# Attention projections: values of two pairs of heads by seven half-depth products, and a pair's last block closed inside the next projection

## The chip, the cores and the metric

The kernel runs on one core of one Trainium2 chip. The metric is the device time of one execution in microseconds (us): before the change the median of three runs is 3855.34 (3853.4 to 3857.73). All arithmetic is f32. The core's engines work side by side, each through its own instructions in order, and wait for each other through semaphores: TensorE (PE in the profile, its weight loads PEld), VectorE (DVE), ScalarE (ACT), GpSimd (POOL) and SyncE (SP, which issues most DMAs).

## The reference, cut to what matters

Four layers of the form x = x + layer(groupnorm(x)) on a 512 x 64 x 64 image: one attention layer, two gated convolution layers, one linear attention. Only the first is touched:

```python
x = x + _L0_conv_ref(_gn(x), wq, wk, wv, wo)

q = to_tokens(_conv1x1(fmap, wq, gain_in))   # 8 heads x 4096 tokens x 64
k = to_tokens(_conv1x1(fmap, wk, gain_in))
v = to_tokens(_conv1x1(fmap, wv, gain_in))
AA = jnp.sum(q * q, axis=-1)
qk = jnp.einsum('bid,bjd->bij', q, k)
sim = -(AA[:, :, None] + AA[:, None, :] - 2.0 * qk) * scale
attn = jax.nn.softmax(sim, axis=-1)
out = jnp.einsum('bij,bjd->bid', attn, v)
return _conv1x1(out.reshape(...), wo, gain_out)
```

## The kernel before

X, the 512 channels x 4096 tokens, stays in SBUF as four chunks of 128 channels. `_attention_pairs` does the eight heads as four pairs; a pair's 2 x 64 channels fill the 128 partitions. Tokens come in NB = 8 blocks of BLK = 512. For each pair there is a projection, `project`, and then the attention proper, block by block.

**Projection.** Four repeats k, of two blocks each, make Q and K of the pair (128 channels x 512 tokens a block). Weights (Q matrix a, K matrix b) times two blocks of X would be eight products of half the depth (256 channels, so two matmuls of 128 x 128 on 512 columns each). `_Seven` does it with seven, in Strassen's manner (Winograd's form): `sums` makes four sums of the two weight matrices (s[0] to s[3]) once a pair, `differences` four differences of the X blocks (t[0] to t[3], eight instructions of VectorE, L450) in every repeat, and `steps` gives the seven products p1, p5, p2, p7, p6, p3, p4 with their evictions. p1 and p5 open PSUM banks 0 and 1 and are copied by ScalarE into "kept" tiles (L620); p2 and p3 go on adding in the same banks; p7 and p6 use banks 2 and 3, p4 adds to 2. VectorE makes five adds a repeat: kept[1] with p7 (L483), kept[0] with p6 (L487), and three that write Q and K (L647); ScalarE writes the fourth quarter (L645). Banks 0 and 1 lie in the pool `ps_av` and 2 and 3 in `ps_s` (three buffers, one of which is taken by `ps_a` during a projection). The "row" tiles (kept, and avs and rd of the attention) have three buffers, the "pt" tiles (differences, squares, the exponentials) five, the "acc" tiles (weight sums, the fourth difference, the running sums of exponentials) two.

The pair's values are made plainly, turned with tokens on the partitions: `value(b)` (L604) multiplies 128-token slices of X, as the loaded operand, by the pair's value weights (128 columns that stream), 4 slices x 4 chunks = 16 matmuls a block, and ScalarE copies the block to V (L611). `squares` (L627) sums Q squared for AA into `ps_a`; at the end of a projection VectorE transposes it (L674) into A, the bias of the exponentials.

**Attention.** For each block b, 32 key tiles t: `scores` (four 64 x 64 matmuls, L693, and two exponentials on ScalarE, L701), and two tiles later `values` (L713) while VectorE adds the tile into acc (L778). After the last tile avs is gathered from two PSUM tiles av0 and av1 (L783, L788). `close` sums acc over the keys by TensorE (ps_d, L722), takes the reciprocal (L726), writes the normalized output over Q (L727) and checks the sums (L728, L731). A block is closed early in the next block, but a pair's last one right after its loop, ahead of the next projection.

The order on each engine is made by the tile framework's scheduler, by its own estimates; a tile's buffer is handed on when its last reader is through. Weights of a pair (wqkv, L576, one DMA) are loaded when the pair before has finished its projection, and scaled by the normalization's gain (L395 on GpSimd; in pair 0 on VectorE and ScalarE).

Of the kernel before, what the change touches and what calls it, by code (L numbers as in the profile page):

```python
# [143 lines left out]
def _all(pieces):  # L144
    for _ in pieces:
        pass
# [269 lines left out]
class _Seven:  # L416
# [22 lines left out]
    def differences(self, eng, x, t):  # L439

        for j, (a, b) in enumerate(
# [7 lines left out]
            for c in range(2):  # L449
                yield eng.tensor_tensor(t[j][c], a(c), b(c), ALU.subtract)  # L450

    def steps(self, a, b, s, t, x, bank, keep, put):

# [5 lines left out]
        def add(j, w, hs, first):  # L459

            if first:
                ps[j] = bank(j)
            for c in range(2):
                self.matmul(
                    ps[j], w[:, c], hs[c], start=(first and c == 0), stop=(c == 1),
                    skip_group_check=not first,
                )

# [28 lines left out]

        return [p1, p5, p2, p7, p6, p3, p4]


# [7 lines left out]
def _attention_pairs(tc, a, X, QO, gmask, small, centered, stats, mv, okay):  # L508
# [19 lines left out]
    with tc.tile_pool(name="att1", bufs=1) as p1, tc.tile_pool(  # L528
# [34 lines left out]
        K = p1.tile([P, N], FP, tag="K", name="K")  # L563
        V = p1.tile([P, NT, P], FP, tag="V", name="V")
        A = p1.tile([P, NT, 2], FP, tag="A", name="A")
# [6 lines left out]

        def project(pair):

            w = p1.tile([P, 3, NC, P], FP, tag="wqkv", name=f"wqkv{pair}")
            nc.sync.dma_start(out=w, in_=a["L0_wqkv"][pair])  # L576
            for n in range(3):
                centered.scaled(
                    w[:, n], gains[:, min(n, 1)],
                    nc.gpsimd if pair else nc.scalar if n else nc.vector,  # L580
                )
            if pair == 0:
                centered.began()
            Q = QO[pair]
            psa = ps_s.tile([P, 2 * BLK], FP, tag="s", name="ps_a")
            wsum = p2.tile([P, 2 * BLK], FP, tag="acc", name="w_sum").rearrange(
                "p (n c m) -> p n c m", n=4, c=2
            )
            wsum = [wsum[:, n] for n in range(4)]
            sums = seven.sums(nc.vector, w[:, 0], w[:, 1], wsum)  # L590

            def differences(k):
                tiles = [ptp.tile([P, 2 * BLK], FP, tag="pt", name="diff") for _ in range(3)]
                tiles.append(p2.tile([P, 2 * BLK], FP, tag="acc", name="diff"))
                t = [[t[:, ts(c, BLK)] for c in range(2)] for t in tiles]
                return t, seven.differences(
                    nc.vector, lambda c, n: X[:, c, ts(2 * k + n, BLK)], t
                )

            def value(b):  # L600
                ps = ps_s.tile([P, 2 * BLK], FP, tag="s", name="ps_v")[:, 0:BLK]
                for i in range(QT):
                    for c in range(NC):
                        nc.tensor.matmul(  # L604
                            ps[:, ts(i, P)],
                            X[:, c, ts(b * QT + i, P)],
                            w[:, 2, c, :],
                            start=(c == 0),
                            stop=(c == NC - 1),
                        )  # L610
                nc.scalar.copy(V[:, ts(b, QT), :].rearrange("p t d -> p (t d)"), ps)  # L611

            def bank(j):
                if j < 2:
                    return ps_av.tile([P, BLK], FP, tag=f"av{j}", name="ps7")
                return ps_mm.tile([P, BLK], FP, tag="mm", name="ps7")

            def keep(j, ps):
                t = p3.tile([P, BLK], FP, tag="row", name="kept")
                nc.scalar.copy(t, ps)  # L620
                return t

            def squares(k, sq):

                sq = sq.rearrange("p (t j k) -> p j t k", j=4, k=32)
                for j in range(4):
                    nc.tensor.matmul(  # L627
                        psa[ts(j, 32), ts(k, 256)].rearrange("p (t k) -> p t k", k=32),
                        halves,
                        sq[:, j],  # L630
                        start=True,
                        stop=True,
                    )

            late = []
            for k in range(NB // 2):
                if pair == 0:
# [4 lines left out]
                def put(m, n, ps, more):  # L642
                    dst = (K if m else Q)[:, ts(2 * k + n, BLK)]
                    if more is None:
                        nc.scalar.copy(dst, ps)  # L645
                    else:
                        nc.vector.tensor_add(dst, ps, more)  # L647
# [24 lines left out]
            late.pop(0)()  # L672
            at = ptp.tile([P, 2 * BLK], FP, tag="pt", name="at")
            nc.vector.transpose(at, psa)  # L674
            nc.vector.tensor_copy(A, at.rearrange("p (t k) -> p t k", k=32)[:, :, 0:2])
# [31 lines left out]

        def values(av, t, pt):
            for half in range(2):
                keys = slice(half * D, (half + 1) * D)  # L710
                for h in range(2):
                    rows = slice(h * D, (h + 1) * D)
                    nc.tensor.matmul(  # L713
                        av[half][rows, :], V[keys, t, rows], pt[keys, ts(h, BLK)],
                        start=(t == 0), stop=(t == NT - 1),
# [34 lines left out]
        for pair in range(HEADS // 2):  # L750
            project(pair)
            if pair == HEADS // 2 - 1:
# [7 lines left out]
            for b in range(NB):  # L760
# [5 lines left out]
                for t in range(NT + AHEAD):  # L766
# [4 lines left out]
                    if t >= AHEAD:  # L771
                        u = t - AHEAD
                        pt = pts.pop(u)
                        values(av, u, pt)
                        if u == 0:
# [1153 lines left out]
```

## Time and profile before

| | |
|---|---|
| median of three runs | 3855.34 us |
| the profiled execution | 3857.97 us, span 3856.2 us |
| granted TensorE clock | 0.997 of full |
| TensorE busy in the span | 3774.7 us, 98% |
| projection of pair 0, of pairs 1 to 3 | about 34 to 116 us; 567.7 to 647.6, 1098.3 to 1178.2, 1629.0 to 1708.9 us |
| attention of pairs 0 to 3 | between these, about 450 us each, the last to about 2250 with the output projection |
| VectorE and ScalarE busy from 566 to 648 us | 37.0 and 16.8 us of 82 |
| the three later layers | about 2274 to 3856 us |

The page gives for each group of instructions its line, engine, output and inputs, count, busy time, mean duration, and the idle time of the engine just before them with what ended it. In a timeline a row is the start in us, the length in us, and the instructions run together. Each f32 matmul leaves two matmul records and two weight load records. Matmul lengths overlap, so the pace is read from the starts.

### The profile page before, as it was taken

What the parts mean: (1) busy time and instruction counts of PE and PEld (TensorE: products, weight loads), DVE (VectorE), ACT (ScalarE), POOL (GpSimd) and SP (SyncE); (2) the same over time, 40 slices, a digit from 0 to 9 for tenths busy, and PEclk for the clock granted to TensorE, in tenths of its full rate; (3) what the DMA queues carried; (4) which work ended last, traced back from release to release, by engine and by line L of the source; (5) the groups of instructions that cost most, each with busy time, mean ns of one, the idle gap of its engine ahead of it and who ended that gap; (6) DMA issues with size and microseconds to landing.
All of it is one profiled execution on the core that took longest, in us unless ns stands there. A gap on an engine that the chain in (4) does not pass through costs nothing. (4 is left out here: it accounts for less than half of the span.)

```text
span 3856.2 us, 81818 instructions
## 1 busy us (share of the span) xinstructions
PE 3774.7 (98%) x35446; PEld 1675.2 (43%) x35446; DVE 2645.7 (69%) x3214; ACT 2067.8 (54%) x2994; POOL 108.6 (3%) x92
## 2 busy tenths in 40 slices
PE   6999999999999999999999999999999999999999
PEld 4533335333354333353333334554444544455544
DVE  5677774777766787747776757767677677575535
ACT  3677763777736777636565655663246632354210
POOL 0000000000000000000000000000000000121100
PEclk9999999999999999999999999999999999999999
DMA  2000000000000000000000015763047730563334
GB/s 99 10 1 1 1 1 9 1 1 1 1 1 9 1 1 1 1 9 1 1 1 1 1 49 161 202 197 84 13 156 193 202 97 27 154 183 92 94 97 140
DMA packets 194012, 221.56 MB, mean 57 GB/s; under 512 B 13400, under 2 KB 138584, under 8 KB 193520
## 3 DMA queue, kind: packets, MB, share of 16 engines
q1 hardware_dynamic: 166832, 157.12, 15.0%
q10 hardware_dynamic: 26784, 59.11, 4.2%
q8 instruction: 280, 4.59, 0.5%
q14 instruction: 84, 0.69, 0.1%
q0 software_dynamic: 32, 0.06, 0.0%
HBM read 156.46 MB, written 59.77 MB: 56 GB/s over the span
## 5 line engine op out<-in xcount | busy, mean ns | idle before, releaser
L701 ACT ACTIVATE pt<-ps_s,A 128x512 f32<-128x512 f32 x2048 | 1286.3, 686 | 534.9 <-PE ps_s L693 527.3
L778 DVE TENSOR_TENSOR acc<-acc,pt 128x1024 f32<-128x1024 f32 x960 | 1178.2, 1227 | 323.5 <-ACT pt L701 296.0
L713 PE MATMUL av<-pt,V 64*64 64x512 f32 x8192 | 1112.6, 590 | 0.9 <-ACT pt L701 0.9
L693 PE MATMUL ps_s<-O,K 64*64 64x512 f32 x8192 | 1111.7, 589 | 0.0
L713 PEld LDWEIGHTS av<-pt,V 64*64 64x64 f32 x8192 | 339.8, 133 | 557.1 <-issue 525.3
L693 PEld LDWEIGHTS ps_s<-O,K 64*64 64x64 f32 x8192 | 334.2, 133 | 554.0 <-issue 307.0
L952 ACT COPY S<-S 32x1295 f32<-32x1295 f32 (+1 forms) x272 | 341.5, 1256 | 219.0 <-DMA S<-F 114.4
L879 PEld LDWEIGHTS ps_cv<-S,T 64*32 64x32 f32 x13824 | 194.0, 105 | 111.1 <-issue 78.7
L879 PE MATMUL ps_cv<-S,T 64*32 64x128 f32 x13824 | 232.6, 273 | 5.8 <-issue 2.1
L879 PE MATMUL ps<-diff,w_sum 128*128 128x512 f32 x492 | 231.7, 602 | 3.1 <-DVE w_sum L437 1.9
L879 PE MATMUL ps<-h,w_out_L 128*128 128x512 f32 x512 | 229.6, 599 | 1.5 <-DVE X L1233 1.4
L450 DVE TENSOR_TENSOR diff<-X 128x512 f32<-128x512 f32 x200 | 133.5, 684 | 73.6 <-PE ps L879 46.9
L879 PE MATMUL ps<-X,w_in_L 128*128 128x512 f32 x304 | 147.1, 615 | 13.3 <-ACT kept L1155 6.3
L383 ACT ACTIVATE X<-X,gn_less 128x512 f32<-128x512 f32 x122 | 77.1, 708 | 152.1 <-DVE gn_less L125 152.1
L879 PEld LDWEIGHTS ps<-h,w_out_L 128*128 128x128 f32 x512 | 94.0, 190 | 118.3 <-issue 96.5
L879 PE MATMUL ps<-h,pw_L 128*128 128x512 f32 x320 | 143.8, 599 | 1.4 <-DVE h L1221 1.1
L1006 DVE STREAM_TRANSPOSE h<-ps_cv 128x512 f32<-128x512 f32 x112 | 109.1, 1047 | 51.4 <-PE ps_cv L879 51.1
L450 DVE TENSOR_TENSOR diff<-X,diff 128x512 f32<-128x512 f32 x200 | 133.6, 683 | 11.6 <-PE ps L879 10.8
L879 PEld LDWEIGHTS ps<-diff,w_sum 128*128 128x128 f32 x492 | 90.3, 190 | 111.4 <-issue 101.5
L604 PEld LDWEIGHTS ps_v<-wqkv,X 128*128 128x128 f32 x1024 | 119.5, 193 | 18.0 <-issue 12.5
L604 PE MATMUL ps_v<-wqkv,X 128*128 128x128 f32 x1024 | 120.8, 276 | 0.0
L483 DVE TENSOR_TENSOR kept<-kept,ps 128x512 f32<-128x512 f32 x57 | 38.9, 682 | 115.8 <-ACT sq L668 77.6
(182 smaller groups left out, 3135.4 us busy)
## 6 DMA issues: line engine op xcount, KB each, us to landing
T<-in_L_T_dram SPq DMA_DIRECT2D x112, 384.0 KB, 4.3
F<-plane ACTq DMA_DIRECT2D x112, 324.0 KB, 3.6
S<-F SPq DMA_DIRECT2D x224, 162.0 KB, 4.5
row<-G SPq DMA_DIRECT2D x80, 272.0 KB, 3.6
S<-G SPq DMA_DIRECT2D x96, 153.0 KB, 4.2
G<-plane ACTq DMA_DIRECT2D x48, 289.0 KB, 2.3
T<-in_L_T_dram SPq DMA_DIRECT2D x48, 256.0 KB, 3.9
out_dram<-y SPq DMA_DIRECT2D x32, 256.0 KB, 2.0
```

The source lines that it names most:

```text
L383: self.nc.scalar.activation(xs, xs, AF.Identity, bias=less)
L450: yield eng.tensor_tensor(t[j][c], a(c), b(c), ALU.subtract)
L483: nc.vector.tensor_add(kept[1], kept[1], ps[2])
L604: nc.tensor.matmul(ps[:, ts(i, P)], X[:, c, ts(b * QT + i, P)], w[:, 2, c, :], start=(c == 0), stop=(c == NC - 1),)
L693: nc.tensor.matmul(ps[ts(half, D), ts(h, BLK)], K[rows, t * P + half * D : t * P + (half + 1) * D], QO[pair][rows, cols], start=True, stop ...
L701: exp = nc.scalar.activation(pt[:, ts(h, BLK)], ps[:, ts(h, BLK)], AF.Exp, bias=A[:, t, h : h + 1])
L713: nc.tensor.matmul(av[half][rows, :], V[keys, t, rows], pt[keys, ts(h, BLK)], start=(t == 0), stop=(t == NT - 1),)
L778: add = nc.vector.tensor_add(acc, acc if u > 1 else first, pt)
L879: self.tc.keep_in_program_order(self.nc.tensor.matmul(*args, **kw))
L952: nc.scalar.copy(second, first)
L1006: nc.vector.transpose(out, src)
```

## The change

- For an even pair the projection makes the values of this pair and the next at once. Two value weight matrices (2 x 128 output channels) on two blocks are again a two by two scheme, so a class `_SevenTurned` runs the same seven steps with the operands swapped: slices of X or of its differences are loaded, weights or their sums stream, 4 x 2 = 8 matmuls of 128 columns a product. Its weight sums lie in the last 1024 columns of the pair's own Q buffer until Q is written there. An odd pair makes no values.
- The values of even pairs lie in QO[3], which is free until pair 3's Q is written; those of odd pairs in V.
- The X differences have one set of tiles a projection, used by both groups of seven and made for repeat k + 1 during the last group of repeat k. Banks 0 and 1 lie in `ps_s` now and 2 and 3 in `ps_av`. `ps_a` is taken after the first repeat.
- Weights come in DMAs of one matrix each; the second value matrix lies in the buffer of the later `wo` tile.
- `close` of a pair's last block is called within the next `project`, after the second product of its first group (except for the last pair, where nothing changes).

The diff, cut to its core:

```diff
+    def multiply(self, ps, w, hs, first):
+        for c in range(2):
+            self.matmul(
+                ps, w[:, c], hs[c], start=(first and c == 0), stop=(c == 1),
+                skip_group_check=not first,
+            )
...
-            for c in range(2):
-                self.matmul(
-                    ps[j], w[:, c], hs[c], start=(first and c == 0), stop=(c == 1),
-                    skip_group_check=not first,
-                )
+            self.multiply(ps[j], w, hs, first)
...
+class _SevenTurned(_Seven):
+    def multiply(self, ps, w, hs, first):
+        for i in range(BLK // P):
+            for c in range(2):
+                self.matmul(
+                    ps[:, ts(i, P)], hs[c][:, ts(i, P)], w[:, c],
+                    start=(first and i == c == 0), stop=(c == 1), skip_group_check=True,
+                )
...
-        def project(pair):
...
+        def home(pair):
+            return V if pair % 2 else QO[NC - 1]
+        def project(pair, meanwhile=None):
             w = p1.tile([P, 3, NC, P], FP, tag="wqkv", name=f"wqkv{pair}")
-            nc.sync.dma_start(out=w, in_=a["L0_wqkv"][pair])
-            for n in range(3):
+            w = [w[:, n] for n in range(3)] + [p1.tile([P, NC, P], FP, tag="wo", name="wv")]
+            src = [(pair, 0), (pair, 1), (pair, 2), (pair + 1, 2)][: 2 if pair % 2 else 4]
+            for n, (p, m) in enumerate(src):
+                nc.sync.dma_start(out=w[n], in_=a["L0_wqkv"][p][:, m])
+            for n in range(len(src)):
                 centered.scaled(
-                    w[:, n], gains[:, min(n, 1)],
-                    nc.gpsimd if pair else nc.scalar if n else nc.vector,
+                    w[n], gains[:, n // 2 if n > 1 else n],
+                    nc.gpsimd if pair else nc.vector if n in (2, 0) else nc.scalar,
                 )
...
-            wsum = p2.tile([P, 2 * BLK], FP, tag="acc", name="w_sum").rearrange(
-                "p (n c m) -> p n c m", n=4, c=2
-            )
-            wsum = [wsum[:, n] for n in range(4)]
-            sums = seven.sums(nc.vector, w[:, 0], w[:, 1], wsum)
+            def matrices(t):
+                t = t.rearrange("p (n c m) -> p n c m", n=4, c=2)
+                return [t[:, n] for n in range(4)]
+            sums = matrices(p2.tile([P, 2 * BLK], FP, tag="acc", name="w_sum"))
+            made = [(w[0], w[1], sums, seven.sums(nc.vector, w[0], w[1], sums))]
+            if pair % 2 == 0:
+                sums = matrices(Q[:, N - 2 * BLK :])
+                made.insert(0, (w[2], w[3], sums, seven.sums(nc.vector, w[2], w[3], sums)))
+            tiles = [ptp.tile([P, 2 * BLK], FP, tag="pt", name="diff") for _ in range(3)]
+            tiles.append(p2.tile([P, 2 * BLK], FP, tag="acc", name="diff"))
+            diff = [[t[:, ts(c, BLK)] for c in range(2)] for t in tiles]
+            def view(k):
+                return lambda c, n: X[:, c, ts(2 * k + n, BLK)]
             def differences(k):
-                tiles = [ptp.tile([P, 2 * BLK], FP, tag="pt", name="diff") for _ in range(3)]
-                tiles.append(p2.tile([P, 2 * BLK], FP, tag="acc", name="diff"))
-                t = [[t[:, ts(c, BLK)] for c in range(2)] for t in tiles]
-                return t, seven.differences(
-                    nc.vector, lambda c, n: X[:, c, ts(2 * k + n, BLK)], t
-                )
-            def value(b):
-                ps = ps_s.tile([P, 2 * BLK], FP, tag="s", name="ps_v")[:, 0:BLK]
-                for i in range(QT):
-                    for c in range(NC):
-                        nc.tensor.matmul(
-                            ps[:, ts(i, P)],
-                            X[:, c, ts(b * QT + i, P)],
-                            w[:, 2, c, :],
-                            start=(c == 0),
-                            stop=(c == NC - 1),
-                        )
-                nc.scalar.copy(V[:, ts(b, QT), :].rearrange("p t d -> p (t d)"), ps)
+                if pair == 0:
+                    for b in (2 * k, 2 * k + 1):
+                        for c in range(NC if b else 0):
+                            centered.take(X[:, c, ts(b, BLK)], c)
+                return seven.differences(nc.vector, view(k), diff)
...
             def bank(j):
                 if j < 2:
-                    return ps_av.tile([P, BLK], FP, tag=f"av{j}", name="ps7")
-                return ps_mm.tile([P, BLK], FP, tag="mm", name="ps7")
+                    return ps_mm.tile([P, BLK], FP, tag="mm", name="ps7")
+                return ps_av.tile([P, BLK], FP, tag=f"av{j - 2}", name="ps7")
...
+            def put(dst, n, ps, more):
+                d = dst[:, ts(n, BLK)]
+                if more is None:
+                    nc.scalar.copy(d, ps)
+                else:
+                    nc.vector.tensor_add(d, ps, more)
+            late, psa = [], []
+            pieces = differences(0)
...
-                    for b in (2 * k, 2 * k + 1):
-                        for c in range(NC if b else 0):
-                            centered.take(X[:, c, ts(b, BLK)], c)
...
-                t, pieces = differences(k)
-                steps = seven.steps(
-                    w[:, 0], w[:, 1], wsum, t, lambda c, n: X[:, c, ts(2 * k + n, BLK)],
-                    bank, keep, put,
-                )
-                value(2 * k)
-                if k:
-                    late.pop(0)()
-                for _ in range(4):
-                    next(sums, None)
-                    next(pieces)
-                    next(pieces)
-                for step in steps[:5]:
-                    step()
-                value(2 * k + 1)
-                for step in steps[5:]:
-                    step()
+                after = iter(())
+                for g, (wa, wb, ws, sums) in enumerate(made):
+                    values = g + 1 < len(made)
+                    dst = [home(pair), home(pair + 1)] if values else [Q, K]
+                    steps = (turned if values else seven).steps(
+                        wa, wb, ws, diff, view(k), bank, keep,
+                        lambda m, n, ps, more: put(dst[m], 2 * k + n, ps, more),
+                    )
+                    for n, step in enumerate(steps):
+                        if n == 0:
+                            next(sums, None)
+                            next(pieces, None)
+                            next(pieces, None)
+                        if n == 1:
+                            _all(sums)
+                            _all(pieces)
+                        step()
+                        if n == 1 and meanwhile:
+                            meanwhile()
+                            meanwhile = None
+                        if n == 3 and late:
+                            late.pop()()
+                        if not values and n == 2 and k + 1 < NB // 2:
+                            pieces = differences(k + 1)
+                        for _ in range(0 if values else {2: 2, 5: 4}.get(n, 0)):
+                            next(pieces, None)
+                if not psa:
+                    psa.append(ps_s.tile([P, 2 * BLK], FP, tag="s", name="ps_a"))
...
-            project(pair)
+            project(pair, pair and (lambda: close(*done)))
...
             if pair == HEADS // 2 - 1:
                 output(NB - 2, range(2))
-            close(*done)
+                close(*done)
```

More of the change, by code (lines that the diff above doesn't have):

```diff
@@ L563, in _attention_pairs @@
         K = p1.tile([P, N], FP, tag="K", name="K")
-        V = p1.tile([P, NT, P], FP, tag="V", name="V")
+        V = p1.tile([P, N], FP, tag="V", name="V")
         A = p1.tile([P, NT, 2], FP, tag="A", name="A")
@@ L571, in _attention_pairs @@
         seven = _Seven(tc, nc.tensor.matmul)
-        def project(pair):
+        turned = _SevenTurned(tc, nc.tensor.matmul)
+        def home(pair):
+            return V if pair % 2 else QO[NC - 1]
+        def project(pair, meanwhile=None):
             w = p1.tile([P, 3, NC, P], FP, tag="wqkv", name=f"wqkv{pair}")
-            nc.sync.dma_start(out=w, in_=a["L0_wqkv"][pair])
-            for n in range(3):
+            w = [w[:, n] for n in range(3)] + [p1.tile([P, NC, P], FP, tag="wo", name="wv")]
[3 more added lines that the diff above has]
+            for n in range(len(src)):
                 centered.scaled(
-                    w[:, n], gains[:, min(n, 1)],
-                    nc.gpsimd if pair else nc.scalar if n else nc.vector,
+                    w[n], gains[:, n // 2 if n > 1 else n],
+                    nc.gpsimd if pair else nc.vector if n in (2, 0) else nc.scalar,
                 )
@@ L584, in project @@
             Q = QO[pair]
-            psa = ps_s.tile([P, 2 * BLK], FP, tag="s", name="ps_a")
-            wsum = p2.tile([P, 2 * BLK], FP, tag="acc", name="w_sum").rearrange(
-                "p (n c m) -> p n c m", n=4, c=2
-            )
-            wsum = [wsum[:, n] for n in range(4)]
-            sums = seven.sums(nc.vector, w[:, 0], w[:, 1], wsum)
-            def differences(k):
-                tiles = [ptp.tile([P, 2 * BLK], FP, tag="pt", name="diff") for _ in range(3)]
-                tiles.append(p2.tile([P, 2 * BLK], FP, tag="acc", name="diff"))
-                t = [[t[:, ts(c, BLK)] for c in range(2)] for t in tiles]
-                return t, seven.differences(
-                    nc.vector, lambda c, n: X[:, c, ts(2 * k + n, BLK)], t
-                )
@@ L627, in squares @@
                     nc.tensor.matmul(
-                        psa[ts(j, 32), ts(k, 256)].rearrange("p (t k) -> p t k", k=32),
+                        psa[0][ts(j, 32), ts(k, 256)].rearrange("p (t k) -> p t k", k=32),
                         halves,
@@ L633, in squares @@
                     )
-            late = []
-            for k in range(NB // 2):
-                if pair == 0:
-                    for b in (2 * k, 2 * k + 1):
-                        for c in range(NC if b else 0):
-                            centered.take(X[:, c, ts(b, BLK)], c)
[L642 to L647, printed above, removed]
-                t, pieces = differences(k)
-                steps = seven.steps(
-                    w[:, 0], w[:, 1], wsum, t, lambda c, n: X[:, c, ts(2 * k + n, BLK)],
-                    bank, keep, put,
-                )
-                value(2 * k)
-                if k:
-                    late.pop(0)()
-                for _ in range(4):
-                    next(sums, None)
-                    next(pieces)
-                    next(pieces)
-                for step in steps[:5]:
-                    step()
-                value(2 * k + 1)
-                for step in steps[5:]:
-                    step()
@@ L671, in project @@
                 late.append(lambda k=k, sq=sq: squares(k, sq))
-            late.pop(0)()
+            late.pop()()
             at = ptp.tile([P, 2 * BLK], FP, tag="pt", name="at")
-            nc.vector.transpose(at, psa)
+            nc.vector.transpose(at, psa[0])
             nc.vector.tensor_copy(A, at.rearrange("p (t k) -> p t k", k=32)[:, :, 0:2])
@@ L706, in scores, with values @@
             return pt
-        def values(av, t, pt):
+        def values(v, av, t, pt):
             for half in range(2):
@@ L713, in values @@
                     nc.tensor.matmul(
-                        av[half][rows, :], V[keys, t, rows], pt[keys, ts(h, BLK)],
+                        av[half][rows, :],
+                        v[keys, t * P + h * D : t * P + (h + 1) * D],
+                        pt[keys, ts(h, BLK)],
                         start=(t == 0), stop=(t == NT - 1),
@@ L773, in _attention_pairs @@
                         pt = pts.pop(u)
-                        values(av, u, pt)
+                        values(home(pair), av, u, pt)
                         if u == 0:
```

## The prediction

> **What bounds the kernel now.** I read the page's first part, then TensorE's waits in the attention stage (34 to 2274 us), then the timelines of the first pair boundary, then one repeat of a projection on each engine, and last the order of the changed kernel's instructions.
>
> Page, busy time by engine; TensorE's waits from 34 to 2274 us (total, times, longest):
>
> ```profile
> PE 3774.7 (98%) x35446; PEld 1675.2 (43%) x35446; DVE 2645.7 (69%) x3214; ACT 2067.8 (54%) x2994; POOL 108.6 (3%) x92
> ```
> ```profile
> PE ps L464 <- issue: 4.5, 1, 4.5
> PE ps_d L722 <- DVE acc L778: 4.2, 3, 1.4
> PE gn_ps L124 <- DVEq L817: 2.8, 1, 2.8
> PE av L713 <- ACT pt L701: 0.9, 1, 0.9
> ```
>
> TensorE is the bound, and in the attention it waits almost only at pair boundaries: three times 1.4 us before ps_d, a pair's last denominators. So matmul time removed here shortens the run, if nothing new is late. TensorE at the first boundary and in the next projection (start, length):
>
> ```profile
> 562.55 2.75 PE L713 MATMUL av<-pt,V 64*64 64x512 f32 x24
> 566.69 1.08 PE L722 MATMUL ps_d<-acc,ones 128*64 128x512 f32 x4 [1.38 <-DVE acc L778]
> 567.70 3.84 PE L604 MATMUL ps_v<-wqkv,X 128*128 128x128 f32 x32
> ...
> 599.88 1.88 PE L464 MATMUL ps<-X,w_sum 128*128 128x512 f32 x4
> 601.60 3.73 PE L604 MATMUL ps_v<-wqkv,X 128*128 128x128 f32 x32
> 605.17 1.88 PE L464 MATMUL ps<-diff,wqkv 128*128 128x512 f32 x4
> 606.89 3.73 PE L604 MATMUL ps_v<-wqkv,X 128*128 128x128 f32 x32
> 610.55 0.64 PE L627 MATMUL ps_a<-sq,halves 128*32 128x256 f32 x8
> 611.12 1.98 PE L464 MATMUL ps<-X,wqkv 128*128 128x512 f32 x4
> ```
>
> Starts count, since lengths overlap. A half-depth product of Q and K (4 records; each f32 matmul leaves two) takes 601.60 - 599.88 = 1.72. A block of values (32 records) takes 605.17 - 601.60 = 3.57, or 112 ns a record. The four ps_a products take 0.57. One repeat: 610.55 to 630.48 = 19.93. A projection from its first product to the scores takes 79.90 in pairs 1, 2 and 3 (567.70 to 647.60, 1098.33 to 1178.23, 1628.96 to 1708.86).
>
> The groups of the second projection show the eviction prices:
>
> ```profile
> L604 PE MATMUL ps_v<-wqkv,X 128*128 128x128 f32 x256 | 30.1, 276 | 0.0
> L611 ACT COPY V<-ps_v 128x512 f32<-128x512 f32 x8 | 4.7, 586 | 35.5 <-PE ps_v L604 35.5
> L726 DVE RECIPROCAL rd<-ps_d 128x512 f32<-128x512 f32 x1 | 3.3, 3347 | 0.0
> L647 DVE TENSOR_TENSOR K<-ps,kept 128x512 f32<-128x512 f32 x4 | 2.8, 692 | 9.6 <-PE ps L464 9.6
> ```
>
> TensorE never waits there; VectorE and ScalarE do. A copy is 0.59, a VectorE add 0.69 (0.60 from start to start in a row).
>
> **The change, part by part.**
>
> *Values of two pairs.* For two pairs and two blocks, the old form has 2 x 2 x 3.57 = 14.28 us of matmul, which is eight half-depth products of 1.785. The new form has seven with the same operands' roles (a 128-column slice of X or a difference is loaded, a 128-column weight streams), so I price them by the same row: 12.50. One product is saved in each of 4 repeats x 2 even pairs = 8, that is 128 of 1024 records: 8 x 1.785 = **14.3 us**. Bounds: at the Q/K rate (1.72) the seven would cost 0.07 less each, 56 x 0.07 = 3.9 more gain; at the dearer value block (606.89 to 610.55 = 3.66, half 1.83) 56 x 0.045 = 2.5 less. I take 1.785, the same form in the middle of its stream. The Trainium skill (TensorE: Matmul & The Clock Gate, Back-to-back issue gap) puts about 81 ns on a 128-column matmul in a stream of loads and products, which taken record for record would make the 128 worth 10.4 us, an estimate; the 112 ns row is this very form and decides.
>
> A repeat is 0.2 more than its parts (19.93 against 7 x 1.72 + 2 x 3.57 + 0.57 = 19.75), at the two ends of ps_a (3.66 before it, 1.82 after it). ps_a stays once a repeat, so I leave the 0.2; bounds 16 x 0.1 = 1.6 either way.
>
> New repeats: even pairs 12.50 + 7 x 1.72 + 0.57 + 0.2 = 25.3 us, odd pairs the same without the values, 12.8.
>
> *Evictions.* Eight repeats gain 5 VectorE adds each (40 x 0.69 = 27.6 us) and 8 sums of weights (3.3 us); ScalarE has 24 copies for 32. Cover is TensorE: an even repeat has 18 VectorE instructions, 18 x 0.60 = 10.9 us in 25.3; an odd one 13, 7.9 in 12.8. I replayed the new order with the rows above, counting 0.2 us from a product's end to its eviction. Odd repeat, started at 0: p3 ends at 10.9, its add (PSUM bank 1) at 12.4, and the next p5 wants that bank at 14.5; p4's add ends at 14.1, wanted at 18.0 by the next p7. Differences are now one set, not a new one each repeat: t[0] is rewritten after p5 and t[3] after p4, and each is done over 1 us before its reader. Even repeats have more slack. So nothing on the path; if cover fails, each microsecond over the 2 us of slack counts up to 24 times, once a group.
>
> *Last block closed later.* After the last av product TensorE goes straight to p1 and p5: their differences and sums are in VectorE's order ahead of the last acc, as now, and finished by about 565.4. The three waits of 1.4 go: 4.2. ps_d itself (1.0) stays. What is late next is the 3.35 us reciprocal: it now stands on VectorE between the group's first evictions. Odd boundary: it runs 12.9 to 16.2 after p1's start; behind it K's add (16.9) frees both the bank of p7 and a "row" buffer for the next p1's copy. TensorE has finished p5 of the second repeat at 16.5; the order puts half of p7 first, which starts at 16.9: 0.46 lost, in two boundaries. Even boundary: bank 1 comes free at 15.45, wanted at 15.2: 0.25 lost. Sum 1.2. Bounds: 0, and the whole reciprocal each time, 10. I take 1.2, so the gain is **3.0**.
>
> *Weights.* Eleven loads of 256 KB (four of 768 KB before). In pair 0 VectorE scales two matrices ahead of the first product in place of one: 0.60 more, **0.6** lost (0 to 1.3). ScalarE's copies stand among its 0.62 us shifts of X: p1's copy ends at 39.1 and p2 wants it at 40.0, so nothing more.
>
> One new wait has a queue behind it: after pair 1's projection the sums of pair 2's weights stand on VectorE ahead of the first acc add, and wait for GpSimd's third scaling, which waits for the load. Queued behind are the acc adds, which free the pt buffers (five) that exp needs. GpSimd's scalings of today (start, length):
>
> ```profile
> 119.88 4.02 POOL L395 TENSOR_TENSOR wqkv<-wqkv,gains 128x512 f32<-128x512 f32 x3 [90.11 <-ACT pt L701]
> 652.09 5.75 POOL L395 TENSOR_TENSOR wqkv<-wqkv,gains 128x512 f32<-128x512 f32 x3 [528.19 <-DMA wqkv<-in_L_wqkv_dram]
> ```
>
> With E the end of the projection's last product (646.9 in pair 1), the load is in and scaling starts at E + 5.2. One scaling takes 1.04 us with VectorE idle (the shortest of the nine) and 2.02 beside it. VectorE will be idle, waiting: third scaling at E + 8.3, three sums 9.5, first acc add done 10.8. exp of t = 5, the first that needs a buffer back, starts at E + 9.1 now, so it would be 1.7 late; TensorE needs its result only 2.0 us after it is made (values run two tiles behind scores). Cost 0. Bounds: 0, and with 5.75 us of scaling 5.2 + 5.75 + 1.3 + 1.2 - 9.1 - 2.0 = 2.3. The Trainium skill (SBUF — State Buffer, Who interferes with whom) says that a VectorE instruction with two SBUF inputs and a GpSimd one that reads SBUF exclude each other; that speaks against putting more two-input work on VectorE, and by it the wait sits on the cheap side, 1.04, since the waiting engine holds nothing.
>
> **Sum.** 14.3 + 3.0 - 0.6 = 16.7 us. The profiled execution took 3857.97 (span 3856.2 and 1.8 around it), 2.6 over the median of 3855.34, within the spread of the three runs. Profiled: 3841.3; as a median: 3855.3 - 16.7 = **3838.6**.
>
> **Rivals.**
> 1. *Forecast*: 3832 to 3843, by the rate bounds and part of the others. 0.70.
> 2. *It is done, but a part is eaten*: the boundaries pay nothing (3.0), the scaling wait costs 2.3 and the values go at 1.83 (2.5): 3838.6 + 7.8 = 3846. For it: only three "row" buffers and a 3.35 us reciprocal in front of evictions. 0.15.
> 3. *Eviction takes the matmuls' place* (and the change does not do what it says): the value blocks were 3.6 us pauses in which VectorE caught up; without them TensorE waits for banks in every group. 0.7 us in each of 24 groups (16 of Q and K, 8 of values) is 16.8: 3855. Against it: 2 us of slack in the replay, and evictions that now wait for TensorE. 0.07.
> 4. *Slower*: the turned products' loads are no longer hidden, since the streamed operand is a sum just written, in the output's own buffer, and the order changes every 16 records. One load takes 192 ns alone (the ps_v load group); 896 records at 192 instead of 112 are 72 us: 3838.6 + 72 = 3911. It decides from 112 + 16.7/896 = 131 ns on. Against it: the ps_v rows hide the same loads at 112. 0.04.
> 5. More than forecast, under 3832 (values at the Q/K rate, ps_a's ends gone, new waits nil): 0.04.
>
> **Numbers.** Likeliest 3838.6. The range goes from 3832 to 3848, rival 2 inside; left out are most of 3, 4 and 5. About 0.2% (7.7 us) is what a measurement can tell here: faster means under 3847.6. Faster 0.88, same 0.08, slower 0.04.
>
> **What would show it.** In the changed profile: 896 value records at 112 ns from start to start, under ps groups that load X or diff and stream O or wqkv; even repeats of 25.3 and odd of 12.8 us; no wait before ps_d; waits of 0.5 us or less for VectorE in a projection's second repeat; VectorE about 31 us busier; the first scores of pair 0 some 22 us later and of pair 1 some 8 us earlier than now (115.6 and 647.6). Wrong if turned records come over 120 ns apart, if a wait of TensorE for kept, ps or diff returns with every repeat, or if exp stands still after pair 1's projection.

## The result, and the profile after

The changed kernel takes 3838.7 us in the median of six runs (3836.33 to 3840.77), the kernel before 3855.55 beside it (3853.4 to 3857.73). The ratio is 0.9956, 95% interval 0.9945 to 0.9966. The profiled execution took 3836.61 us (span 3834.9).

The page's busy times by engine, after:

```profile
PE 3757.4 (98%) x35318; PEld 1659.6 (43%) x35318; DVE 2671.5 (70%) x3263; ACT 2063.7 (54%) x2986; POOL 102.5 (3%) x91
```

TensorE has 128 records less and is 17.3 us less busy; the span is 21.3 shorter. TensorE's waits from 34 to 2274 us (total, times, longest):

```profile
PE ps L511 <- DVE wqkv L395: 5.1, 1, 5.1
PE ps L911 <- ACT w_in_L L391: 4.0, 1, 4.0
PE gn_ps L124 <- DVEq L849: 2.8, 1, 2.8
PE gn_ps L132 <- DVE gn_d L129: 1.8, 1, 1.8
PE av L743 <- ACT pt L731: 0.9, 1, 0.9
```

The three waits before ps_d are gone, and no wait of a product for a bank, a kept tile or a difference has come. (L911, L124 and L132 belong to the next layer, which now starts inside the window.) TensorE at the first boundary and in the odd projection behind it (start, length):

```profile
585.35 2.75 PE L743 MATMUL av<-pt,O 64*64 64x512 f32 x24
588.04 1.98 PE L454 MATMUL ps<-X,wqkv 128*128 128x512 f32 x4
589.86 1.88 PE L454 MATMUL ps<-diff,w_sum 128*128 128x512 f32 x4
591.67 1.08 PE L754 MATMUL ps_d<-acc,ones 128*64 128x512 f32 x4
592.68 1.98 PE L454 MATMUL ps<-X,wqkv 128*128 128x512 f32 x4
...
601.36 1.88 PE L454 MATMUL ps<-X,wqkv 128*128 128x512 f32 x4
603.08 2.74 PE L454 MATMUL ps<-diff,w_sum 128*128 128x512 f32 x6
```

From the start of the last av products to the next work are 2.69 us where there were 4.14. ps_d stands between two products without a wait, and the second repeat passes the place where I expected a stall (604.8, in the x6 row) without one. One even repeat, from p1 of the values at 1114.47 to the next at 1139.76:

```profile
1114.47 1.95 PE L511 MATMUL ps<-wqkv,X 128*128 128x128 f32 x16
1116.26 1.95 PE L511 MATMUL ps<-O,diff 128*128 128x128 f32 x16
1118.04 1.95 PE L511 MATMUL ps<-wqkv,X 128*128 128x128 f32 x16
1119.83 1.95 PE L511 MATMUL ps<-O,diff 128*128 128x128 f32 x16
1121.71 0.64 PE L650 MATMUL ps_a<-sq,halves 128*32 128x256 f32 x8
...
1139.76 1.95 PE L511 MATMUL ps<-wqkv,X 128*128 128x128 f32 x16
```

A turned product is 1.785 from start to start (1116.26 to 1119.83 are two), 112 ns a record, and the repeat 25.29; an odd one (614.15 to 626.93) takes 12.78.

**A finer mark than the total.** After the attention the instructions are the same in every kernel here, yet they took between 1576.4 and 1586.0 us in the twelve profiled executions. So I compare the moment at which the attention ends: GpSimd's first work of the next layer, "MEMSET plane", waits for it in every kernel. It starts at 2273.64 before and at 2256.26 after: 17.4 us earlier.

```profile
2273.64 1.22 POOL L873 MEMSET plane<- 128x648 f32 x2 [1086.28 <-DVEq L817]
2256.26 1.22 POOL L905 MEMSET plane<- 128x648 f32 x2 [1060.79 <-DVEq L849]
```

This mark has a scatter of its own: a slow beginning of TensorE, told of below, moves it by up to 1 us between executions of the same instructions.

### The profile page after: what moved, and what is told of

Read it like the earlier page. It is cut to its first block, busy times and chain, and to the rows that moved or that the text cites. A ratio compares the mean times of both kernels' runs of the same rounds, so it can differ in the third digit from the quotient of the medians.

```text
span 3834.9 us, 81658 instructions
## 1 busy us (share of the span) xinstructions
PE 3757.4 (98%) x35318; PEld 1659.6 (43%) x35318; DVE 2671.5 (70%) x3263; ACT 2063.7 (54%) x2986; POOL 102.5 (3%) x91
## 5 line engine op out<-in xcount | busy, mean ns | idle before, releaser
L743 PE MATMUL av<-pt,O 64*64 64x512 f32 x4096 | 558.2, 590 | 0.9 <-ACT pt L731 0.9
L743 PE MATMUL av<-pt,V 64*64 64x512 f32 x4096 | 554.3, 590 | 0.0
L743 PEld LDWEIGHTS av<-pt,O 64*64 64x64 f32 x4096 | 171.4, 133 | 276.1 <-issue 255.0
L743 PEld LDWEIGHTS av<-pt,V 64*64 64x64 f32 x4096 | 168.2, 133 | 281.1 <-issue 270.4
L911 PEld LDWEIGHTS ps_cv<-S,T 64*32 64x32 f32 x13824 | 192.3, 105 | 110.2 <-issue 76.4
L911 PE MATMUL ps_cv<-S,T 64*32 64x128 f32 x13824 | 230.8, 272 | 5.5 <-issue 2.0
L911 PE MATMUL ps<-diff,w_sum 128*128 128x512 f32 x492 | 231.1, 601 | 4.6 <-DVE w_sum L437 1.9
L911 PE MATMUL ps<-h,w_out_L 128*128 128x512 f32 x512 | 229.6, 600 | 1.5 <-DVE X L1265 1.4
L911 PE MATMUL ps<-X,w_in_L 128*128 128x512 f32 x304 | 147.9, 619 | 11.9 <-ACT kept L1187 6.7
L911 PEld LDWEIGHTS ps<-h,w_out_L 128*128 128x128 f32 x512 | 94.0, 190 | 118.3 <-issue 96.5
L911 PE MATMUL ps<-h,pw_L 128*128 128x512 f32 x320 | 143.6, 599 | 1.4 <-DVE h L1253 1.1
L911 PEld LDWEIGHTS ps<-diff,w_sum 128*128 128x128 f32 x492 | 90.0, 190 | 112.5 <-issue 102.6
L911 PE MATMUL vkp<-kT,vT 128*128 128x512 f32 x256 | 115.4, 593 | 2.8 <-DVE vT L1669 2.1
```

Source lines behind the costliest of these rows:

```text
L743: nc.tensor.matmul(av[half][rows, :], v[keys, t * P + h * D : t * P + (h + 1) * D], pt[keys, ts(h, BLK)], start=(t == 0), stop=(t == NT - 1),)
L911: self.tc.keep_in_program_order(self.nc.tensor.matmul(*args, **kw))
```

## The experiments

| kernel | attention ends, us | first scores of pairs 0 to 3, us |
|---|---|---|
| before | 2273.64 | 115.61, 647.60, 1178.23, 1708.86 |
| after | 2256.26 | 138.49, 640.38, 1191.00, 1691.60 |
| after, once more | 2256.57 | 138.81, 640.68, 1191.31, 1691.91 |
| 1 closing later alone | 2270.46 | 116.31, 647.04, 1176.42, 1705.79 |
| 2 values by seven alone | 2260.11 | 138.47, 641.61, 1193.49, 1695.44 |
| 3 eight products | 2270.84 | 145.92, 647.81, 1205.59, 1706.19 |
| 4 value matrices first (two executions) | 2255.49, 2255.70 | 137.64 and 137.84, ... |
| 5 bank 1 late | 2280.97 | 137.38, 647.50, 1203.81, 1711.79 |
| 6 bank 2 late | 2279.77 | 138.76, 647.77, 1204.81, 1710.55 |
| 7 one load | 2255.67 | 137.82, 639.71, 1190.41, 1691.01 |
| 8 longer wait | 2267.96 | 137.96, 644.48, 1199.69, 1703.30 |

(In experiment 5 the scheduler put the first scores ahead of the projection's last ps_a products, so its last column is not to be compared with the others.)

**1. The closing alone**, in the kernel before:

```diff
-            project(pair)
+            project(pair, pair and (lambda: close(*done)))
...
+                    if n == 1 and meanwhile:
+                        meanwhile()
+                        meanwhile = None
...
             if pair == HEADS // 2 - 1:
                 output(NB - 2, range(2))
-            close(*done)
+                close(*done)
```

> The kernel before, with one part of the change alone: a pair's last block is closed after p5 of the next projection; values, banks and loads stay as before. Theory (the closing pays by itself): the three waits of 1.4 us before ps_d go and no stall of more than 0.3 us takes their place, so attention ends 3 to 4 us earlier than in the kernel before, of which 4.2 is waits and up to 1 is given back in extra turnarounds. My recorded step says 3.0 (4.2 less 1.2 of stalls behind the reciprocal). Rival (the wait only changes its place): TensorE stands 1 to 3 us at each boundary behind evictions that queue after the 3.35 us reciprocal; attention ends within 1 us of before, or later by up to 6.

Measured: attention ends 3.2 us earlier; 3851.6 against 3854.24, ratio 0.9992 (0.9983 to 1.0001). TensorE's waits in the attention, of which the line for ps_d is gone:

```profile
PE ps L464 <- issue: 4.5, 1, 4.5
PE av L716 <- ACT pt L704: 0.9, 1, 0.9
```

From one pair's first scores to the next pair's it is 1.26, 1.25 and 1.26 us shorter (531.99 against 530.73, and so on): 3.77. The other 0.6 was lost before any boundary: the first scores came 0.70 later by the same instructions, 0.15 of it before the first product (the last section says where the rest is from). So the theory holds: 1.45 of wait goes at each boundary, and 0.2 comes back.

**2. The values alone**, in the changed kernel:

```diff
-            project(pair, pair and (lambda: close(*done)))
+            project(pair)
...
-                close(*done)
+            close(*done)
```

> The changed kernel, with a pair's last block closed at the pair's end again, as before: the values of two pairs by seven alone. Theory (the parts add): the three waits of 1.4 us before ps_d are back, attention ends 3 to 4.5 us later than in the changed kernel, and 13 to 14 us earlier than in the kernel before. Rival (the parts depend on each other: the closing inside the projection delays evictions of the new groups, or hides what the new groups lose): the difference from the changed kernel is under 1 us, or over 6.

Measured: attention ends 3.85 us later than in the changed kernel and 13.5 earlier than before; 3838.64, ratio to before 0.9963 (0.9949 to 0.9977). The waits are back as they were:

```profile
PE ps_d L754 <- DVE acc L810: 4.2, 3, 1.4
```

The closing is worth 3.77 in one kernel and 3.85 in the other, so the parts add.

**3. Eight products**, in the changed kernel: the values of both pairs made plainly, everything else kept.

```diff
-            if pair % 2 == 0:
-                sums = matrices(Q[:, N - 2 * BLK :])
-                made.insert(0, (w[2], w[3], sums, seven.sums(nc.vector, w[2], w[3], sums)))
...
+                if pair % 2 == 0:
+                    for m in range(2):
+                        for n in range(2):
+                            value(m, 2 * k + n)
```

> The changed kernel in all its arrangement (loads, homes of the values, banks, the closing inside the projection), with the values of both pairs of an even projection made plainly: eight half-depth products in place of seven, copied by ScalarE, with no sums of value weights and none of the 40 adds of VectorE. Theory (the whole gain of this part is one product of 1.785 us saved eight times, and the 40 adds and 8 sums are hidden): even repeats of 27.1 us in place of 25.3, attention ends 14.3 us later than in the changed kernel (13.8 to 14.8). Rival (a part of the seven's gain is eaten by evictions): less than 13 us later, and the plain blocks show no waits where the seven show some. Rival (turned products of seven are dearer than plain blocks): records of plain blocks closer than 112 ns from start to start.

Measured: attention ends 14.58 later; 3851.81, ratio to before 0.9995 (0.9986 to 1.0004). Between the first scores of pairs 1 and 2 are 557.78 against 550.62: 7.16, four times 1.79. The plain blocks in it (64 records from one start to the next):

```profile
1123.69 7.31 PE L637 MATMUL ps_v<-wqkv,X 128*128 128x128 f32 x64
1130.84 7.31 PE L637 MATMUL ps_v<-wv,X 128*128 128x128 f32 x64
1137.99 1.88 PE L454 MATMUL ps<-X,wqkv 128*128 128x512 f32 x4
```

7.15 by 64 is 112 ns, as in the turned products, and neither form waits. The whole value of the seven is the eighth product: 40 more adds and 8 sums on VectorE cost nothing that the mark shows. Both rivals fall.

**4. The value matrices first**, in the changed kernel:

```diff
-            for n, (p, m) in enumerate(src):
+            turn = (0, 1) if pair % 2 else (2, 3, 0, 1)
+            for n in turn:
+                p, m = src[n]
...
-            for n in range(len(src)):
+            for n in turn:
```

> The changed kernel, with the four weight matrices of an even pair loaded and scaled in the order of use (the two value matrices first). Theory (the first product of all waits for VectorE's second scaling because the value matrix comes behind the Q matrix): in pair 0 VectorE's scaling for the first product is its first, TensorE's first product comes 0.6 to 0.9 us earlier than in the changed kernel (35.09 us), and as no other thing moves, attention ends 0.6 to 0.9 us earlier. Rival (the first product waits for the second matrix's load, for X's first block or for ScalarE, whichever scaling comes first): first product at 35.1 as now, no gain.

TensorE's wait before its first product, 5.1 in the changed kernel:

```profile
PE ps L511 <- DVE wqkv L395: 4.5, 1, 4.5
```

It is one scaling, 0.6 us, shorter: the theory. The first product itself comes 0.51 earlier (34.58 against 35.09), a little less than foretold, since all that stands ahead of it came 0.09 later in this execution. Attention ends 0.8 earlier, but that proves little: experiment 7, whose first products are those of the changed kernel, ends as early (2255.67), by a shorter slow beginning. The first time its median was 3833.98, 4.7 below the changed kernel's, though the ratio to the kernel before beside it was 0.9955 (0.9941 to 0.9968), no better than the 0.9956 of the changed kernel. So I ran both again side by side:

> The changed kernel with the value matrices loaded and scaled first, again, beside the changed kernel on the same chip. Theory (one scaling, 0.60 us, is all that it saves): 0.5 to 0.9 us less than the changed kernel, which 5 rounds will not tell from nothing. Rival (its median of 3834.0, 4.7 us under the changed kernel's, was no accident): 3 us or more less, outside the spread of both.

> The changed kernel again, beside the one with the value matrices first. Expected as before: 3838.7, ratio to the kernel before 0.9956.

Then they took 3838.81 and 3839.27 (ratios to before 0.9951, 0.9937 to 0.9965, and 0.9953, 0.9940 to 0.9967). The 4.7 did not come again; the later layers alone scatter by more. What is left is the 0.6 us of the first wait, which only the trace can tell: a slightly better kernel, not a measurably faster one.

**5 and 6. One bank late.** An add is preceded by a 3.35 us reciprocal into its destination, for bank 1 in one kernel and for bank 2, with (m, n) == (1, 0), in the other:

```diff
+                if late:
+                    nc.vector.reciprocal(d, ps)
...
-                        lambda m, n, ps, more: put(dst[m], 2 * k + n, ps, more),
+                        lambda m, n, ps, more: put(dst[m], 2 * k + n, ps, more, (m, n) == (0, 1)),
```

> The changed kernel, with a VectorE instruction of 3.35 us (a reciprocal of the bank, into the destination, which the add then overwrites) ahead of the add that empties PSUM bank 1, in all 24 groups of seven. Theory (the evictions have about 2 us of slack: bank 1 in my replay is empty 2.1 us before the next group wants it): of each 3.35 us some 1.3 to 2 become a wait of TensorE in the middle of a projection, and up to 3.3 where the scores come next; together 35 to 50 us later than the changed kernel, and the waits stand before the next group's second product. Rival (the evictions have no slack, each microsecond of VectorE counts): about 80 us later (24 x 3.35). Rival (VectorE is far from mattering): under 15 us.

> The same 3.35 us instruction ahead of the add that empties PSUM bank 2, which by my replay is wanted again 3.9 us after it is empty. Theory (slack of each bank decides): nothing in the middle of a projection (under 0.5 us a group), up to 3.3 us at each of the four ends of a projection, where the scores wait for K; together 0 to 16 us later than the changed kernel. Rival (VectorE's total work decides, whichever bank): the same delay as with bank 1. Rival (no slack at all): about 80 us later.

Measured: 24.7 us later for bank 1 and 23.5 for bank 2; medians 3864.34 and 3862.09, ratios to before 1.0014 (1.0002 to 1.0025) and 1.0010 (0.9999 to 1.0022). Both numbers of my theory missed, the first by too much, the second by too little. The rival that VectorE's total work decides foretold the same delay for both banks, and its number comes close; but 24 reciprocals are 80 us of work, and the waits stand at a few places, not in every group. TensorE's main waits in the attention with bank 1 late:

```profile
PE ps_s L725 <- DVE O L665: 7.4, 4, 1.9
PE ps L454 <- DVE rd L760: 3.7, 2, 1.8
```

and with bank 2 late:

```profile
PE ps_s L725 <- DVE at L706: 8.4, 4, 2.1
PE av L745 <- ACT pt L733: 3.3, 4, 1.3
PE ps L454 <- ACT kept L643: 2.2, 2, 1.1
```

Most of the cost, 18.0 us with bank 1 and 18.3 with bank 2, lies at the four ends of projections, from the last product to the last av record of the pair's first block: there the scores wait. Inside the projections a late bank costs 3.0 and 2.1 us in each of the two odd ones, where the closing's own reciprocal comes on top, 1.2 and 0.8 in pair 2's, and next to nothing in pair 2's later repeats (25.42 us with bank 1, 25.29 with bank 2, as in the changed kernel). For bank 2 that is what the replay said (3.9 us of slack), and in those repeats its products stand in an unchanged order. For bank 1 it does not test the 2.1: from the second repeat of an even pair on, the scheduler had put half of p6 and part of p2 in front of p5, which wants the bank, so the order was another. But the changed kernel's own rows show this slack, here in its first odd projection:

```profile
612.63 0.69 DVE L663 TENSOR_TENSOR O<-ps,kept 128x512 f32<-128x512 f32 x1
615.86 1.88 PE L454 MATMUL ps<-diff,w_sum 128*128 128x512 f32 x4
```

Bank 1 is empty at 613.32, and the next p5 starts in it at 615.86, 2.5 us later.

At the ends the cost is more than the wait. After three of the four ends in each kernel the granted clock (last but two in a row: PEclk) fell. Here is the second end with bank 2 late, where TensorE waits 2.11 and 1.25 us between 649.7 and 654.2:

```profile
653.00:654.00 1.00, 0.00 (x0) 0.00 (x0) 1.00 (x4) 0.57 (x1) 0.28 (x1) 1.00 0.00 0
654.00:655.00 1.00, 0.83 (x5) 0.44 (x9) 0.41 (x2) 1.00 (x3) 0.00 (x0) 0.89 0.00 0
655.00:656.00 1.00, 1.00 (x8) 0.51 (x7) 0.12 (x1) 1.00 (x3) 0.00 (x0) 0.50 0.00 0
656.00:658.00 2.00, 2.00 (x13) 1.02 (x9) 1.90 (x2) 1.00 (x2) 0.00 (x0) 0.50 0.00 0
```

By the trace's record of the clock it stood at half for 6.8 us after the first end and for 3.4 us after two others, in both kernels: 13.7 us, of which half, 6.8 us, is lost if TensorE was busy throughout (an estimate).

**7. One load** of three matrices in pair 2, as before the change:

```diff
+            if pair == 2:
+                nc.sync.dma_start(out=w0, in_=a["L0_wqkv"][pair])
             for n, (p, m) in enumerate(src):
-                nc.sync.dma_start(out=w[n], in_=a["L0_wqkv"][p][:, m])
+                if pair != 2 or n == 3:
+                    nc.sync.dma_start(out=w[n], in_=a["L0_wqkv"][p][:, m])
```

> The changed kernel, with the first three matrices of pair 2 in one load of 768 KB as before the change, in place of three of 256 KB. It tries the step in which I let the load arrive 5.2 us after the projection's last product (as in the kernel before) and found exp of the sixth key tile 1.7 us late, hidden. In the changed kernel the scaling starts 3.0 us after that product. Theory (the smaller loads land earlier): with one load GpSimd's scalings start at about 5.2 us after the last product of pair 1's projection, the weight sums of VectorE at about 8.2, and the first add of the exponentials' sum about 2 us later than in the changed kernel; exp of the sixth tile is 1 to 2 us later, TensorE stands 0 to 0.5 us, and attention ends within 0.5 us of the changed kernel. Rival (loads land when the buffer comes free, whatever their size): scaling still at 3.0. Rival (the delay is not hidden): attention ends 1.7 us or more later.

GpSimd's scalings after pair 1's projection in the changed kernel, whose last product ended at 639.7,

```profile
642.74 3.04 POOL L395 TENSOR_TENSOR wqkv<-wqkv,gains 128x512 f32<-128x512 f32 x3 [498.92 <-DMA wqkv<-in_L_wqkv_dram]
```

and with one load, where it ended at 639.0:

```profile
643.63 4.01 POOL L395 TENSOR_TENSOR wqkv<-wqkv,gains 128x512 f32<-128x512 f32 x3 [500.63 <-DMA wqkv<-in_L_wqkv_dram]
```

Scaling starts 4.6 us after the last product in place of 3.0, so the smaller loads do land earlier. VectorE's sums follow at 8.7 in place of 6.1. exp of the sixth tile starts 9.1 us after in both kernels, and attention ends at 2255.67: no cost. But the scheduler had put one acc add ahead of the sums here, so a late exp, which I thought hidden, was not produced; that it would have been hidden stays untested.

**8. A longer wait before ps_d**, in the kernel of experiment 2:

```diff
+            else:
+                nc.vector.tensor_tensor(acc, acc, acc, ALU.max)
             close(*done)
```

> The kernel with the values of two pairs by seven alone (a pair's last block closed at the pair's end), with one more VectorE instruction of some 1.2 us on acc (the larger of acc and itself, which changes nothing) between the last add and the denominators of pairs 0 to 2, so that TensorE's three waits of 1.4 us before ps_d become about 2.6 to 3.2. It tries what such a wait costs beyond its own length. Theory (a wait costs its length): attention ends 3.6 to 5.4 us later than without the instruction. Rival (a wait of over about 2 us also brings TensorE's clock down to half for up to 3.4 us, as after the 1.85 and 2.1 us waits before the scores in the two kernels with late banks): up to 1.7 us more at each boundary, 5 to 10.5 us in all, with a granted clock under 1.00 in the slices after the wait.

Measured: the three waits are 9.4 us together in place of 4.2, attention ends 7.85 later (from the first scores on, which came 0.5 earlier, 8.4); 3851.72 in the median, beside 3839.27 for the changed kernel. By pairs, from first scores to first scores, 3.38, 3.33 and 1.66 us are lost. At the first boundary the clock, in slices from 590 to 596 us:

```profile
590.00:591.00 1.00, 0.31 (x2) 0.23 (x4) 1.00 (x2) 0.00 (x0) 0.00 (x0) 1.00 0.03 8
591.00:592.00 1.00, 1.00 (x5) 0.28 (x2) 1.00 (x3) 0.00 (x0) 0.00 (x0) 0.81 0.00 0
592.00:593.00 1.00, 1.00 (x2) 0.48 (x3) 1.00 (x2) 0.00 (x0) 0.00 (x0) 0.50 0.00 0
593.00:594.00 1.00, 1.00 (x2) 0.41 (x2) 1.00 (x1) 0.00 (x0) 0.00 (x0) 0.50 0.00 0
594.00:595.00 1.00, 1.00 (x2) 0.34 (x1) 1.00 (x1) 0.00 (x0) 0.00 (x0) 0.50 0.00 0
595.00:596.00 1.00, 1.00 (x3) 0.38 (x2) 1.00 (x2) 0.59 (x1) 0.00 (x0) 0.99 0.00 0
```

Half clock for about 3.4 us: the four records from 591.72 took 3.45 us, 1.73 more than the usual 1.72. The first two boundaries lost 1.7 of wait and 1.7 of clock; the third, where the clock stayed at 1.00 and the records at their usual pace, 1.7 of wait alone. The rival holds.

## Why the prediction was right, step by step

The forecast (3838.6) and its mechanism hold; 16.7 us were predicted and the attention ends 17.4 earlier. But three terms were off by 0.7 to 0.8 us each, two one way and one the other; that the sum is nearer than its terms is partly luck.

- *Values, 14.3.* Right: 112 ns a record and 25.29 and 12.78 us a repeat; undoing it costs 14.58, of which 14.32 in its steady form (2 x 7.16).
- *ps_a's 0.2 a repeat, 0 with bounds of 1.6.* Mis-sized a little: with eight products in the new order, an even and an odd projection without ps_d take 159.43 us against 2 x 79.90 before (109.51 from the first product to the scores in experiment 3, less 1.2 for ps_d and its turnarounds, and 51.13 in experiment 2). So the order itself gains some 0.4 every two pairs, 0.7 in all.
- *Evictions, 0.* Right in what they cost (experiment 3, no waits), and the slack of bank 2 held (experiment 6); that of bank 1 is 2.5 where I had 2.1. (18 x 0.60 is 10.8 and 13 x 0.60 is 7.8, each 0.1 less than I wrote; nothing hangs on it.) VectorE is 25.8 us busier, where I counted 31: its adds over acc took 5.4 us less (1213.6 against 1219.0).
- *Closing, 3.0.* Right in kind, mis-sized: 3.8. The waits gave 1.45 each; the stalls of 0.46 and 0.25 behind the reciprocal did not come, and 0.2 of turnaround at each ps_d, which I had not counted, did. The reciprocal ran from 12.7 to 16.0 us after p1's start, not 12.9 to 16.2, and K's add was done at 16.55, just ahead of TensorE, which wanted the bank at 16.76:

```profile
600.70 3.35 DVE L758 RECIPROCAL rd<-ps_d 128x512 f32<-128x512 f32 x1
603.96 0.63 DVE L663 TENSOR_TENSOR K<-ps,kept 128x512 f32<-128x512 f32 x1
```

  A margin of 0.2 us: the next microsecond there would cost, as experiments 5 and 6 show.
- *Weights at the start, 0.6.* Right for what it counted (first product 0.86 later, 0.21 of it lost ahead of this code; experiment 4 takes the 0.6 out of the wait again). There are twelve loads of 256 KB, not eleven, which changes nothing. But another 0.8 went, for which there was no term: pair 0's projection takes 103.40 us from its first product, 2.25 more than pair 2's without ps_d; before, 81.38 and 1.48 more. That is TensorE's slow beginning:

```profile
35.09 3.75 PE L511 MATMUL ps<-wqkv,X 128*128 128x128 f32 x16 [5.13 <-DVE wqkv L395]
38.64 2.54 PE L511 MATMUL ps<-O,diff 128*128 128x128 f32 x16
41.01 1.95 PE L511 MATMUL ps<-wqkv,X 128*128 128x128 f32 x16
```

  3.55 and 2.37 for products of 1.785. The trace's record of the clock begins, with full clock, at 39.87 us here and at 37.31 before, 4.77 and 3.07 us after the first product; half of that, 2.39 and 1.54, is nearly what was lost. It is no cost of the change, since it varies between executions of the same instructions: 3.30 us in experiment 7 and 5.57 in the changed kernel once more, with first scores at 137.82 and 138.81. Mainly for this reason pair 0's first scores came 22.9 us later and pair 1's 7.2 earlier, not 22 and 8.
- *GpSimd's wait, 0 by cover.* The 0 was right by luck, and the way to it wrong: I took the landing of the one load of before (5.2 us after the last product) for the smaller ones, which land by 3.0. So the first add over acc was done 8.3 us after it, not 10.8, ahead of exp's 9.1; no cover was needed:

```profile
646.82 1.22 DVE L810 TENSOR_TENSOR acc<-pt 128x1024 f32<-128x1024 f32 x1
648.84 1.27 ACT L731 ACTIVATE pt<-ps_s,A 128x512 f32<-128x512 f32 x2 [0.45 <-PE ps_s L723]
```

  That a scaling costs 1.04 beside a waiting VectorE was right: 3.04 for three here, 4.01 in experiment 7 with one add beside them. This agrees with the Trainium skill (SBUF — State Buffer, Who interferes with whom), by which an add with two SBUF inputs and a GpSimd instruction that reads SBUF exclude each other.

Together: 14.3 + 0.7 + 3.8 - 0.65 - 0.2 - 0.8 = 17.2, of 17.4 measured. Of the rivals, a part eaten, evictions as the bound and loads no longer hidden are each excluded by the absence of waits and by 112 ns a record.

## What to carry to other kernels

Where one engine is busy 98% of a stage, a saved instruction is worth its start-to-start pace times its count, if a replay of the other engines finds every new eviction early; check the replay at the stage's ends, since there the slack ends first. Take a transfer's landing from one of the same size. To judge an edit of a few microseconds, compare the moment at which its stage ends in the trace: the total scattered by up to 9.6 us here through later work that nobody had touched.

## What the runs showed of the hardware that was not expected

A wait of TensorE can cost more than its length. After waits of 1.4 us (before, and experiment 2) the records kept their pace. After 3.12 us the granted clock fell to 0.50 for 3.4 us at two of three boundaries, which made the price 1.7 us more; after 1.85 us (experiment 5), or 2.11 with a second gap of 0.4 to 1.3 behind it (experiment 6), at three of four ends of projections. Two waits of 1.84 in the middle of a projection (experiment 5) left the pace as it was.

The traces show in part why some waits of one length brought the clock down and others did not. In each trace the recorded clock changes only at whole multiples of 3.41 us from its first entry. In experiment 8 the two waits that lowered it lay with 2.5 and 2.6 of their 3.1 us within one such stretch (588.20 to 591.61 and 1093.37 to 1096.78), and the clock fell at the end of it. The third lay across a border at 1649.75, 1.7 us ahead of it and 1.4 behind; so did the waits at the two ends in experiments 5 and 6 after which the clock stayed. How much idle time in a stretch is enough stays open: 1.4 us in one stretch was enough at the third end in experiment 5, and was not at the second boundary before the change, nor were 1.8 us in the middle of a projection. The Trainium skill (TensorE: Matmul & The Clock Gate, What's actually happening) has a monitor with a free-running window of about 3.4 us that halves the clock after an idle window. That fits the stretches, the length of the slow spells and that they come at some boundaries only; that a wait of 2.1 us, well under a window, is enough at some places, the rule as stated does not say, and the runs do.

At the start of the kernel TensorE's records ran at half pace until the record of the clock begins, 2.9 to 5.6 us after the first product in the twelve executions; the clock column reads 1.00 there, but only because nothing is recorded yet. In eleven of the twelve the time that pair 0's projection takes longer than the same instructions in steady work is half of that stretch, within 0.2 us (experiment 5, with its other order, is the twelfth). The first 32 records of values took 4.17 us before and 4.72 in experiment 1, where full clock began at 37.31 and 38.62 and the instructions up to there are the same. That is the 0.55 by which experiment 1 seemed to fall short.
